# An attention pair: the next image's projection moved between the last weighted sums, bursts placed anew, and casts given to GpSimd

## The chip, the core and the metric

The kernel runs on one core of a Trainium2 chip. The core has a matrix engine (PE, whose weight loads are listed as PEld), a vector engine (DVE), a scalar engine (ACT), GpSimd (POOL), and SyncE (SP), which here only issues transfers. The metric is the device time of one execution in microseconds. Seven executions of the kernel before took 2803.36 to 2808.71 us, with a median of 2805.67.

## The reference

Eight images of 512 channels and 32x32 tokens (T = 1024) pass through two attention layers.

```python
# layer 0, 8 heads of 64 channels
h   = group_norm(x)                       # 32 groups
qkv = qkv_w @ h + qkv_b
q, k, v = split per head, each fake_quant to 8 bits over the whole tensor
w   = softmax(q k / 8);  a = w v          # per head, 1024 x 1024
x   = x + proj_w @ a + proj_b
# layer 1, one head of 512 channels
h = group_norm(x);  q, k, v = wq h, wk h, wv h
o = softmax(q k / sqrt(512)) v
x = x + wp @ o + bp
```

The range of the quantization is that of all images together, so all of q, k and v of layer 0 must be known before the first softmax.

## The kernel before

**Stages.** The first stage (to 627 us) computes q, k and v of layer 0 for all images and writes them to DRAM. The second one does the attention of image 0 alone (to 794 us), with folded weights for layer 1 being computed beside it. In the third one layer 1 of image b runs together with layer 0's attention of image b + 1. The last image's layer 1 ends the program.

**Attention of layer 0** is the generator `attention` (L744). A unit is a head pair's tile of 128 keys by 512 queries. For a unit, PE makes two score matmuls (`st`), ACT takes the exponential of the tile into `pt` (L768), a cast to 16 bits makes its high part `two[:, 0]` (L777), and DVE's subtraction makes the low part (L778). From both parts PE computes weighted sums (`av`) and row sums (`sm`). One step of the generator does four units; the text calls it a burst. It makes the scores of four units to come, two of them at its start and two in its middle or end, and the weighted and row sums of the four units that the burst before has prepared. The casts and subtractions of a burst's last two units are put off as a chore (`later("sum", ...)`) and issued at the next occasion, at the latest when the next burst begins. Score tiles (`st`) come from a PSUM pool of two double banks, `ps_s` (L631); `av` and `sm` from `ps_v`; the banks of layer 1 from `ps_o`. There are three `pt` buffers (L640).

The engine of the cast depends on where the burst is: while image 0 is alone, odd units go to DVE; in a *dense* burst (one that `others` asked for with a negative yield) the two late units go to GpSimd and DVE; all others go to ACT.

**Layer 1** is the generator `others` (L1447). For image b it runs `project` (L908; attention output times the projection weights, plus x, with the statistics of the norm taken on the way), `norm1` (L948) and `layer1` (L1243). Products are done in blocks by a scheme of seven half-sized products (`seven`, L986). A block has two PSUM banks x and y. Products 0, 2, 4 and 5 go one upon the other into x, and between them ACT copies out what x holds (`keep`); DVE adds such copies to y (`add`). After each product the block yields its step number. Layer 1 of an image has, in this order, the blocks a_block (half 0), v_block2 (0 and 1), s_block (0 and 1), o_run (half 0), a_block (half 1), s_block (0 and 1) and o_run (half 1). Products of o_run are twice as long as the others. Before its third product, o_run adds up the softmax's row sums with PE (`sm_l`), which needs DVE's sum `acc`.

**Who sets the order.** The main loop asks `others` for a step and, after each of its yields, does one burst. So the places of `yield` in `others`, `run` (L1232) and `o_run` (L1140) set where bursts lie. Before the change every block yields at step 5, o_run also at step 3, the projection between its halves, and the norm three times with -1 (dense). That makes 16 bursts per image, as many as an image of layer 0 has. `LEAD` (L42) bursts are done ahead, before layer 1 begins. Matmuls run in the order in which they are written; for the other engines a scheduler fixes an order when the program is built.

For the last image alone, `project` and `norm1` already run inside the o_run of the image before it, between its steps 4 and 6 (L1321 to L1331), with banks of `ps_v`. For all other images they come after that o_run, and the image's norm is followed by its first block.

**Loads.** The projection's weights and x of the next image are loaded by ACT's queue just before the last o_run of an image (L1313, L1314), x in eight transfers (`load_x2`, L882).

Of the kernel before, what the change touches and what calls it, by code (L numbers as in the profile page):

```python
# [40 lines left out]
ALIKE = 8.0  # L41
LEAD = 3  # L42
IN_ORDER = mybir.DependencyInfo(mybir.DependencyClass.NoSync, mybir.DependencyReason.DATA)
# [10 lines left out]
def attn_pair_kernel(  # L54
# [126 lines left out]
    flag = const.tile([P, 1], I32, name="flag")  # L181
    off = const.tile([P, 1], F32, name="off")

    with ExitStack() as fast:
# [4 lines left out]
        def av_bank(name):  # L189
            return ps_v.tile([P, 512], F32, tag="v", name=name)  # L190

        def bank(name):
# [551 lines left out]
        def attention():  # L744
# [10 lines left out]
            def scores(u, wait=False):  # L755
                b, j, hf, s = units[u]
                if hf == 0 and s == 0:
                    settle("quant")
                nm = f"{b}_{j}_{hf}"
                qt, kt, _ = pairs[b, j]  # L760
                st = pair_ps(f"st_{nm}_{s}")
                for i, r in enumerate(HALF):
                    mm(
                        st[:, i, :], lhsT=kt[r, bass.ts(s, P)],
                        rhs=qt[r, bass.ts(hf, 512)], start=True, stop=True,
                    )
                pt = ptp.tile([P, 2, 512], F32, tag="p", name=f"pt_{nm}_{s}")
                nc.scalar.activation(pt, st, AF.Exp, scale=esc)  # L768
                parts[u] = two = partp.tile([P, 2, 2, 512], F16, tag="two", name=f"two_{nm}_{s}")
                cast = nc.scalar.copy  # L770
                if alone and s % 2:
                    cast = nc.vector.tensor_copy
                elif dense and wait and not alone:
                    cast = nc.vector.tensor_copy if s % 2 else nc.gpsimd.tensor_copy

                def split():
                    cast(two[:, 0], pt)  # L777
# [75 lines left out]
            for u in range(0, len(units), 4):  # L853
                b, j, hf, s = units[u]
                settle("sum")
                if hf == 0 and s == 0:
                    n = b * PAIRS + j + 1
                    if n < B * PAIRS:
                        pairs[divmod(n, PAIRS)] = load_pair(*divmod(n, PAIRS))

                if u + 4 < len(units):
                    scores(u + 4)
                    scores(u + 5)
                weighted((u, u + 1))
                late = dense
                for n in range(2):
                    if n == late:
                        weighted((u + 2, u + 3))  # L870
                        if s == NT - 4:
                            finish(b, j, hf)
                    if n == 0 and u + 4 < len(units):
                        scores(u + 6, wait=True)
                        scores(u + 7, wait=True)
                chore(0)
                last = (j, hf, s) == (PAIRS - 1, NH - 1, NT - 4)
                yield 6.0 + (hf == NH - 1 and s == NT - 4), b + last
# [3 lines left out]
        def load_x2(b, dma):  # L882

            xts[b] = l1p.tile([P, CC, T], F32, tag="h", name=f"h2_{b}")
            for hf in range(NH):
                for oc in range(CC):
                    dma(
                        xts[b][:, oc, bass.ts(hf, 512)], x_v[b, :, oc, bass.ts(hf, 512)]
                    )

# [17 lines left out]
        def project(b, bank=bank):  # L908
# [6 lines left out]
            for hf in range(NH):  # L915
# [16 lines left out]
                if hf + 1 < NH:  # L932
                    yield 1
            for k in [k for k in ao if k[0] == b]:
# [40 lines left out]
        def inverse1(b, hf, acc):  # L975
            nm = f"l1_{b}_{hf}"
            sm = row_sums([acc[:, bass.ts(i, P)] for i in range(4)], lambda nm: pair_ps(nm)[:, 0, :], nm)
            rs = l1p.tile([P, 512], F32, tag="rs1", name=f"rs1_{b}_{hf}")
# [161 lines left out]
        def o_run(b, hf, vt, vs, ps_, pts, acc, rx, between):  # L1140
# [46 lines left out]
            for step in seven(  # L1187
# [4 lines left out]
            ):  # L1192
                if step == (3 if final else 2):
                    settle("acc")
                    rs = inverse1(b, hf, acc)
                if step == (4 if final else 3):
                    yield 1
# [4 lines left out]
                elif step == 5:  # L1202
                    if not final:
                        finish(2)
                    yield from between[1]()
                    yield 1
                elif step == 6:
                    for n in ((0, 2, 3) if final else (3,) if spare else ()):
                        finish(n)
                    settle("o")  # L1210
                    yield from between[2]()
                    if final and hf == NH - 1:
                        check_sums()
                    if (1, 0) not in rx:
                        load_x1(b, hf, 1, 0, rx)
# [15 lines left out]

        def run(*blocks):  # L1232

            for steps in zip(*blocks):
                if steps[0] == 5:
                    yield 1
# [6 lines left out]
        def layer1(b, steps):  # L1243

            for _ in steps:
# [5 lines left out]
            def a_run(hf):  # L1253
                gq = l1p.tile([P, 7, CC // 2, 256], F32, tag="g", name=f"g_{b}_{hf}")
                yield from run(a_block(b, hf, gq))
                return gq
# [22 lines left out]
            for hf in range(NH):  # L1279
# [55 lines left out]
        def fold():  # L1335
# [16 lines left out]
            def through(i):  # L1352
# [8 lines left out]
                widen(wide[:, i], z)  # L1361


            tiny = small.tile([P, 32], F16, tag="tiny", name="tiny")
            nc.vector.tensor_scalar(tiny, ones[:, 0:32], 2.0**-20, None, ALU.mult)
            ps = bank("tiny")
            for i in range(4):
                mm(ps[32 * i : 32 * i + 32, 0:32], lhsT=ones16, rhs=tiny, start=True, stop=True)
            nc.vector.tensor_scalar(off, ps[:, 0:1], 2.0**-13, None, ALU.not_equal)

# [34 lines left out]
        def check_sums():  # L1405
# [12 lines left out]
            nc.vector.tensor_scalar(bad[:, 0:1], bad[:, 0:1], -1.0, 1.0, ALU.mult, ALU.add)  # L1418
            nc.vector.tensor_max(bad[:, 0:1], bad[:, 0:1], off)
            nc.vector.tensor_reduce(bad[:, 1:2], rcs[:, NR0:], AX.X, ALU.max)  # L1420
# [417 lines left out]
```

## Time and profile before

| | |
|---|---|
| seven executions, median | 2805.67 us |
| the profiled execution | 2807.82 us |
| its span, first to last instruction | 2806.0 us |
| granted PE clock | 0.990 of full speed |
| PE busy | 2641.8 us |
| DVE busy | 1879.1 us |
| ACT busy | 1305.4 us |
| GpSimd busy | 74.7 us |
| casts of `two` on ACT, DVE, GpSimd | 430, 61, 21 |
| their mean time there | 1.07, 0.68, 2.50 us |

A line of a timeline gives the start and the length in us, the engine, the line of the kernel, the operation, the tile written and those read, the shapes, and how many instructions in a row were merged; the square bracket gives the idle time of the engine before it and what ended it. A line of the windows gives the window, its length, and the busy time of each engine with the number of its instructions; then the granted clock, the share of the DMA engines' time and GB/s. Matmuls overlap, so the distance of two starts tells more than a matmul's length. PE runs a float32 matmul as two instructions, so counts on it are twice those in the code.

### The profile page before, as it was taken

Reading aid. Unit: us, or ns where it says so; the run is one execution under the profiler, and the core shown is the slowest. Engines: PE = TensorE matmul, PEld = TensorE weight load, DVE = VectorE, ACT = ScalarE, POOL = GpSimd, SP = SyncE. Lnnn points to the kernel's source line nnn. Section 1 sums busy time; section 2 is a strip of 40 time slices with the busy share of each in tenths; the row PEclk is TensorE's granted clock in tenths of the full one; section 3 lists DMA queues with packets and bytes.
Section 4 is the critical chain, followed back from the end, with each engine's and each line's share of the span. In section 5 each row is a group of like instructions: output and inputs, shape, how many; then the busy total and the mean of one; then the engine's idle time right before and its main releaser. Section 6 shows DMA issues by size and latency. Waiting matters only on the chain.

```text
span 2806.0 us, 33124 instructions
## 1 busy us (share of the span) xinstructions
PE 2641.8 (94%) x13114; PEld 1634.8 (58%) x13114; DVE 1879.1 (67%) x2798; ACT 1305.4 (47%) x1648; POOL 74.7 (3%) x51
## 2 busy tenths in 40 slices
PE   7999999997789999999999999999999999899998
PEld 3455555552236664666466556646664666466687
DVE  6766665658986667666865676667667666755534
ACT  0011111117965665655566566556664665565021
POOL 0000000000000001000100010001001000100000
PEclk9999999999899999999999999999999999999999
DMA  5233232323321233124202411331232124202401
GB/s 195 101 120 120 111 114 90 120 110 130 100 94 31 65 99 101 46 65 132 82 26 65 158 50 39 98 129 31 65 102 99 46 65 136 65 1 54 143 8 43
DMA packets 148228, 241.93 MB, mean 86 GB/s; under 512 B 27360, under 2 KB 92896, under 8 KB 146528
## 3 DMA queue, kind: packets, MB, share of 16 engines
q1 hardware_dynamic: 116544, 181.50, 19.6%
q10 hardware_dynamic: 31520, 58.23, 6.3%
q8 instruction: 104, 1.70, 0.3%
q14 instruction: 60, 0.49, 0.1%
HBM read 152.86 MB, written 86.28 MB: 85 GB/s over the span
## 4 chain that ended last, share of the span: by engine, by line
PE 55%; DVE 17%; ACT 14%; issue 9%; DMA 4%; POOL 1%; ACTq 0%; SPq 0%; DVEq 0%; POOLq 0%
PE s L106 12%; PE qkps L106 10%; PE o L106 9%; ACT pt L768 7%; PE pj L106 7%; DVE two L778 6%; PE v2ps L106 5%; PE vps L106 5%; ACT two L777 4%; PE av L106 2%; PE g L106 2%; PE st L106 1%; PE sm L106 1%; DVE acc L1294 1%; DMA raw<-k_d 1%
## 5 line engine op out<-in xcount | busy, mean ns | idle before, releaser
L778 DVE TENSOR_TENSOR two<-pt,two 128x1024 f16<-128x1024 f32 x512 | 612.5, 1221 | 199.6 <-ACT two L777 199.0
L768 ACT ACTIVATE pt<-st,esc 128x1024 f32<-128x1024 f32 x512 | 554.0, 1128 | 198.3 <-PE st L106 182.7
L777 ACT CAST two<-pt 128x1024 f16<-128x1024 f32 x430 | 441.2, 1067 | 1.3
L106 PE MATMUL av<-two,v 128*64 128x512 f16 x2048 | 279.3, 394 | 1.6 <-DVE two L778 0.8
L396 ACT ACTIVATE u<-qkps,qkb 128x512 f32<-128x512 f32 x84 | 57.8, 688 | 476.5 <-PE qkps L106 467.5
L106 PE MATMUL s<-g,h 128*128 128x256 f32 x1024 | 237.4, 382 | 14.9 <-ACT p L1123 7.9
L106 PE MATMUL st<-q,k 64*128 64x512 bf16 x1024 | 173.6, 388 | 70.8 <-ACT pt L768 69.4
L106 PE MATMUL pj<-ao,wp 128*128 128x512 f32 x512 | 223.3, 594 | 0.1
L106 PEld LDWEIGHTS s<-g,h 128*128 128x128 f32 x1024 | 191.8, 190 | 50.4 <-ACT p L1123 10.3
L106 PEld LDWEIGHTS <-v 128*64 128x64 f16 x2048 | 97.9, 110 | 155.8 <-issue 105.1
L106 PE MATMUL s<-g,sums 128*128 128x256 f32 x768 | 179.8, 384 | 1.1 <-ACT kept_u L1094 0.7
L106 PE MATMUL o<-p,v 128*128 128x256 f32 x768 | 173.9, 383 | 5.6 <-ACT p L1123 5.6
L106 PE MATMUL qkps<-x,wqkv 128*128 128x512 f32 x352 | 164.7, 611 | 2.6 <-DVE x L155 2.6
L106 PEld LDWEIGHTS pj<-ao,wp 128*128 128x128 f32 x512 | 96.5, 190 | 119.5 <-issue 114.7
L106 PEld LDWEIGHTS o<-p,v 128*128 128x128 f32 x768 | 143.6, 190 | 35.1 <-ACT p L1123 10.8
L106 PE MATMUL sm<-two,ones 128*32 128x512 f16 x2048 | 162.3, 395 | 0.0
L106 PEld LDWEIGHTS s<-g,sums 128*128 128x128 f32 x768 | 142.4, 190 | 28.7 <-issue 6.3
L106 PEld LDWEIGHTS <-k 64*128 64x128 bf16 x1024 | 38.6, 94 | 202.6 <-issue 201.9
L106 PE MATMUL qkps<-sums,wa 128*128 128x512 f32 x336 | 153.3, 592 | 0.0
L106 PE MATMUL g<-h,wa 128*128 128x256 f32 x512 | 123.1, 389 | 15.4 <-DVE g L1070 8.2
L106 PE MATMUL v2ps<-wm,h 128*128 128x256 f32 x512 | 119.4, 382 | 6.9 <-ACT g L1057 5.3
L1127 DVE TENSOR_TENSOR p<-s,kept_u 128x512 f32<-128x512 f32 x90 | 61.7, 685 | 93.0 <-ACT kept_u L1094 86.1
(222 smaller groups left out, 3476.1 us busy)
## 6 DMA issues: line engine op xcount, KB each, us to landing
rs<-rs_d SPq DMA_DIRECT2D x80, 256.0 KB
x<-in_x_dram SPq DMA_DIRECT2D x32, 512.0 KB
raw<-q_d SPq DMA_DIRECT2D x32, 512.0 KB
raw<-k_d SPq DMA_DIRECT2D x32, 512.0 KB
raw<-v_d SPq DMA_DIRECT2D x32, 512.0 KB
x_d<-h SPq DMA_DIRECT2D x64, 256.0 KB
x<-x_d ACTq DMA_DIRECT2D x64, 256.0 KB
out_dram<-x SPq DMA_DIRECT2D x64, 256.0 KB
```

Source lines behind the costliest of these rows:

```text
L106: ins = nc.tensor.matmul(*args, **kw).ins
L396: nc.scalar.activation(dst, x, AF.Identity, bias=bias)
L768: nc.scalar.activation(pt, st, AF.Exp, scale=esc)
L777: cast(two[:, 0], pt)
L778: nc.vector.tensor_tensor(two[:, 1], pt, two[:, 0], ALU.subtract)
L1127: tt(dst, ps, u, ALU.add)
L1294: later("acc", 0, lambda two=two: tt(acc, *two, ALU.add))
```

## The change

- In every image's last o_run, between its steps 4 and 6, the next image's projection and norm are done (only image 0's stay in front). Their PSUM tiles are taken from the scores' pool `ps_s`.
- The norm no longer yields, except for image 0's. The bursts that were there are placed elsewhere: v_block2 (0) at step 3, v_block2 (1) at steps 1 and 5, the s_blocks of half 0 at 3 and at 1 and 5, those of half 1 and the a_block of half 1 at step 3, o_run at steps 3 and 6, the second one also at 1, and one, now dense, between the halves of the projection.
- Outside the stage of image 0 alone, the cast of every odd unit is done by GpSimd, that of every even one by ACT.
- A burst that is not dense does the weighted sums of all four units and then their row sums, instead of two units at a time.
- `LEAD` is 2. x is loaded in two transfers. A test of how PE treats very small 16-bit numbers (`tiny`, `off`) is dropped.

```diff
-LEAD = 3
+LEAD = 2
...
+        def score_bank(name):
+            return pair_ps(name)[:, 0, :]
...
                 cast = nc.scalar.copy
-                if alone and s % 2:
-                    cast = nc.vector.tensor_copy
-                elif dense and wait and not alone:
-                    cast = nc.vector.tensor_copy if s % 2 else nc.gpsimd.tensor_copy
+                if s % 2:
+                    cast = nc.vector.tensor_copy if alone else nc.gpsimd.tensor_copy
...
-                weighted((u, u + 1))
+                weighted((u, u + 1) if dense else range(u, u + 4))
                 late = dense
                 for n in range(2):
                     if n == late:
-                        weighted((u + 2, u + 3))
+                        if dense:
+                            weighted((u + 2, u + 3))
...
             for hf in range(NH):
-                for oc in range(CC):
-                    dma(
-                        xts[b][:, oc, bass.ts(hf, 512)], x_v[b, :, oc, bass.ts(hf, 512)]
-                    )
+                dma(xts[b][:, :, bass.ts(hf, 512)], x_v[b, :, :, bass.ts(hf, 512)])
...
                 if hf + 1 < NH:
-                    yield 1
+                    yield -1
...
-                if step == (3 if final else 2):
+                if step == 1 and hf == NH - 1:
+                    yield 1
+                elif step == (3 if final else 2):
                     settle("acc")
                     rs = inverse1(b, hf, acc)
-                if step == (4 if final else 3):
+                elif step == 3:
                     yield 1
...
                     yield from between[1]()
+                elif step == 6:
+                    yield from between[2]()
                     yield 1
-                elif step == 6:
                     for n in ((0, 2, 3) if final else (3,) if spare else ()):
                         finish(n)
                     settle("o")
-                    yield from between[2]()
...
-        def run(*blocks):
+        def run(*blocks, at=(5,)):
 
             for steps in zip(*blocks):
-                if steps[0] == 5:
+                if steps[0] in at:
                     yield 1
...
-                yield from run(a_block(b, hf, gq))
+                yield from run(a_block(b, hf, gq), at=(3,) if hf else (5,))
...
-                yield from run(*(v_block2(b, n, vt) for n in ns))
+                yield from run(*(v_block2(b, n, vt) for n in ns), at=(1, 5) if NH - 1 in ns else (3,))
...
-                    yield from run(*(s_block(b, hf, n, gq, pts, gather) for n in ns))
+                    yield from run(
+                        *(s_block(b, hf, n, gq, pts, gather) for n in ns),
+                        at=(1, 5) if NH - 1 in ns and hf == 0 else (3,),
+                    )
...
-                if b == B - 2 and last:
+                if b + 1 < B and last:
 
                     def first():
                         nonlocal ahead
-                        yield from project(b + 1, av_bank)
-                        ahead = norm1(b + 1, av_bank)
+                        yield from project(b + 1, score_bank)
+                        ahead = norm1(b + 1, score_bank)
                         next(ahead)
```

More of the change, by code (lines that the diff above doesn't have):

```diff
@@ L181, in attn_pair_kernel @@
     flag = const.tile([P, 1], I32, name="flag")
-    off = const.tile([P, 1], F32, name="off")
     with ExitStack() as fast:
@@ L976, in inverse1 @@
             nm = f"l1_{b}_{hf}"
-            sm = row_sums([acc[:, bass.ts(i, P)] for i in range(4)], lambda nm: pair_ps(nm)[:, 0, :], nm)
+            sm = row_sums([acc[:, bass.ts(i, P)] for i in range(4)], score_bank, nm)
             rs = l1p.tile([P, 512], F32, tag="rs1", name=f"rs1_{b}_{hf}")
@@ L1361, in through @@
                 widen(wide[:, i], z)
[L1364 to L1369, printed above, removed]
             for i, (rows, lw, rw) in enumerate(((wa_rows, NQ1, NK1), (wm_rows, NV1, WP1))):
@@ L1418, in check_sums @@
             nc.vector.tensor_scalar(bad[:, 0:1], bad[:, 0:1], -1.0, 1.0, ALU.mult, ALU.add)
-            nc.vector.tensor_max(bad[:, 0:1], bad[:, 0:1], off)
             nc.vector.tensor_reduce(bad[:, 1:2], rcs[:, NR0:], AX.X, ALU.max)
```

## The prediction

> **Names.** A *burst* is one step of the attention generator: scores of four tiles (st), weighted sums and row sums of the four before (av, sm). a0, a1, v0, v1, s00, s01, s10, s11, o0, o1 are the blocks of seven products of layer 1 in their order, s01 the second score block of half 0. *Step n* is `yield n` in `seven` (L986). A *round* runs from one image's projection to the next one's.
>
> **What bounds it now.** I read the page first: which engine is full?
>
> ```profile
> PE 2641.8 (94%) x13114; PEld 1634.8 (58%) x13114; DVE 1879.1 (67%) x2798; ACT 1305.4 (47%) x1648; POOL 74.7 (3%) x51
> ```
>
> PE bounds the whole, and no other engine is near full. So the change is worth what it does to PE's own work and to PE's waits. The windows by round (span, then busy time and count of PE, PEld, DVE, ACT, POOL) give a typical round:
>
> ```profile
> 1060.97:1324.39 263.42, 248.55 (x1397) 158.17 (x1396) 179.48 (x236) 158.13 (x198) 9.39 (x4) 1.00 0.26 80
> ```
>
> The idle column of PE's timeline in it adds up to 14.9 us. Next, a burst, in PE's timeline and then in ACT's:
>
> ```profile
> 1139.79 0.61 PE L106 MATMUL st<-q,k 64*128 64x512 bf16 x4
> 1140.33 1.05 PE L106 MATMUL av<-two,v 128*64 128x512 f16 x8
> 1141.31 0.62 PE L106 MATMUL sm<-two,ones 128*32 128x512 f16 x8
> 1141.86 1.05 PE L106 MATMUL av<-two,v 128*64 128x512 f16 x8
> 1142.84 0.62 PE L106 MATMUL sm<-two,ones 128*32 128x512 f16 x8
> 1143.39 0.60 PE L106 MATMUL st<-q,k 64*128 64x512 bf16 x4
> 1143.93 1.99 PE L106 MATMUL v2ps<-wm,sums 128*128 128x256 f32 x8
> ```
>
> ```profile
> 1140.38 2.12 ACT L768 ACTIVATE pt<-st,esc 128x1024 f32<-128x1024 f32 x2
> 1142.38 2.00 ACT L777 CAST two<-pt 128x1024 f16<-128x1024 f32 x2
> 1144.27 2.14 ACT L768 ACTIVATE pt<-st,esc 128x1024 f32<-128x1024 f32 x2
> ```
>
> By the starts the burst takes 4.14 us. Four av pairs take 0.98 and two st pairs 0.54, so a pair is 0.22 and each change of kind costs 0.54 - 0.44 = 0.10. Third, what a block costs that has no burst at step 5 (end of image 6, attention done, ACT idle): product 5 goes on in the bank that step 5's copy (L1017) is still reading.
>
> ```profile
> 2590.21 1.89 PE L106 MATMUL s<-g,h 128*128 128x256 f32 x8
> 2592.83 1.99 PE L106 MATMUL s<-g,sums 128*128 128x256 f32 x8 [0.73 <-ACT kept_u L1094]
> ```
>
> Fourth, GpSimd's few casts in the norm stretch, and what DVE does at the end of the third:
>
> ```profile
> 1104.03 1.04 POOL L777 CAST two<-pt 128x1024 f16<-128x1024 f32 x1 [4.55 <-ACT pt L768]
> 1107.43 1.39 POOL L151 TENSOR_TENSOR grstd_b<-grstd_b,mhalf 128x4 f32<-128x4 f32 x1 [2.36 <-DVE grstd_b L150]
> 1111.79 5.76 POOL L777 CAST two<-pt 128x1024 f16<-128x1024 f32 x1 [2.97 <-ACT pt L768]
> ```
>
> ```profile
> 1115.97 0.68 DVE L972 TENSOR_TENSOR sums<-h,sums 128x512 f32<-128x512 f32 x1
> 1116.58 1.25 DVE L155 TENSOR_SCALAR h<-h,gmean_b,grstd_b 128x512 f32<-128x512 f32 x1
> ```
>
> A cast takes 1.04 where DVE pauses, and 5.76 where DVE runs back to back (it does from 1108.93 on); when the cast gets through, DVE pays: 1.25 where the same instruction takes 0.53 a little later. Fifth, the norm stretch on PE:
>
> ```profile
> 1105.90 0.39 PE L106 MATMUL st<-q,k 64*128 64x512 bf16 x2 [1.03 <-ACT pt L768]
> ...
> 1118.48 1.99 PE L106 MATMUL g<-h,wa 128*128 128x256 f32 x8 [1.21 <-DVE g L1070]
> ```
>
> **What it saves.** The built kernels' static order has 110 bursts beside layer 1 (109 before), 100 of them undivided.
>
> S1. An undivided burst (st, 16 av, 16 sm, st) has two changes of kind less: 4.14 - 0.20 = 3.94; 100 x 0.20 = 20.0.
>
> S2. The norm stretch: from 1092.70 to 1111.09 PE needs 18.4 us for three bursts and two 0.34 matmuls that are 13.1 without waits; with the waits of 0.48 and 1.21 in a0 that is 7.0. It goes for images 1 to 6 (image 7 had it already): 42.0.
>
> S3. Bursts in score blocks take 4.55, as the second exp is behind a cast and a p-exp on ACT. In the new order the odd cast is off ACT: 4 x 0.41 x 7 rounds = 11.5.
>
> S4. Waits at block edges that follow a burst at step 5, where ACT comes late to the last copy: v0-v1 0.23, a1-s10 0.73, s10-s11 1.32 + 0.37, s11-o1 0.49, in a1 0.58, and the second sm_l, which a burst at o1's step 1 will cover, 1.25: 4.97 x 7 = 34.8.
>
> S5. LEAD 2: one burst leaves the stage where ACT sets the pace (764.00 to 771.07 is one burst, 7.07): 3.1.
>
> Sum 111.4.
>
> **What it costs.**
>
> C1. Seven blocks lose their burst at step 5 and wait there for ACT's copy: v0, s00, s10, s11, o0 at 0.73; a1 copies in two activates (0.84 for 0.59): 0.98; in o1 a norm matmul lies in the gap: 0.4. 5.03 x 7 = 35.2.
>
> C2. The same blocks then need step 5's DVE add for product 6, and DVE does the burst's four subtractions (1.14 each) first. Worked out for a burst in whose middle ACT also copies av and sm (L815, L816): exps 0.59 to 2.71, cast to 3.6, copies to 4.6, exps to 6.7, cast to 7.75; DVE's third and fourth subtraction to 10.1, the add to 10.75. PE: 3.94 + 2 x 1.78 (products 3, 4), copy to 8.25, product 5 to 10.03. Late by 0.75: v0, s11; 0.5 in a1; in v1 (step 1) 0.55 at product 3; in s00 two quantizations (0.74) come between: 0.4, or 1.4 if the odd cast then waits for DVE; I take 1.1. 3.65 x 7 = 25.6; from 10.5 (half of the late adds hidden) to 62 (each behind one more cast of 1.05).
>
> C3. v1-s00 0.85 for 0.26; s01 has two bursts, the second in the old ACT order, its last st 0.9 late; a0-v0 0.5 better; the first sm_l: between s01's first burst and it DVE has eight subtractions, 11 us of other work and two odd casts that it must let through, which makes 3.1 of the 1.59. 2.5 x 7 = 17.5; 10 to 25.
>
> C4. The projection in o1 uses the scores' two buffers: in its burst the second st waits for DVE's evacuation of the last pj (0.75 + 0.2, less the first st): 0.8; at step 6 it waits for grstd: 0.84. Then a0: DVE has the norm (four 0.48, sums 0.6 each), two subtractions and one odd cast ahead of o1's last add, which frees a0's second bank: 2.05, and 0.35 two products on. 4.05 x 6 = 24.3; 10 (a0 hidden by product 6) to 33.
>
> C5. Image 0 keeps its norm stretch, with one cast more on ACT per burst: 0.95 x 3 = 2.9; 0 to 6.
>
> C6. A cast that starts just ahead of a DVE instruction holds it up; the row is 0.72. Six adds a round end waits of PE; for half of them: 2.1 x 7 = 14.7; 0 to 44 (1.05 for each).
>
> Sum 120.2, between 66 and 205. No end can be excluded: the trace of before never has a cast on GpSimd beside a score or o block. I take the middle values, nearer to the 5.76 row than to the 1.04 row wherever DVE runs back to back.
>
> By the Trainium skill (SBUF — State Buffer, SBUF: two separate sides) the port pair that DVE and GpSimd share goes whole to whichever starts first, so a cast should be late by one DVE instruction at most: 1.04 + 1.22 = 2.3 us, an estimate. With that the odd-cast shares of C2 to C4 would go (about 18 us), and the sum would end at 2797. The row of 5.76 behind some seven DVE instructions says otherwise.
>
> **Costed at nothing.** The loads of x: eight issues on ACT (4.14 us together at 2597.96) become two; at 0.53 each, as the two-run load of x1, ACT is free 3 us sooner in o1, but PE's next wait there was DVE's. They must land 22 us before the projection needs them (three o products of 3.56, sm_l and two bursts, one product more); at image 6 the projection came 16 us after the first issue and waited for nothing. If late, up to 5 us a round. GpSimd's pow comes behind one cast (1.04), in C4. The dropped `off` test is four matmuls and some DVE work at 625: under 1 us. On SP the projection's eight stores of x1 (0.32 each, L930) now stand among o1's stores of out; behind them wait the next pair's raw loads, needed a burst later: at most 1 us a round, taken as nothing.
>
> **Sum.** The profiled execution took 2807.82 (span 2806.0 and 1.8 around it), 2.15 over the median of 2805.67. 2807.8 - 111.4 + 120.2 = 2816.6; against the median, 2814.5.
>
> **Rivals.** A measurement of this kernel tells about 0.2% from no change, that is 2800 to 2811.
>
> *Faster:* casts slip into DVE's pauses (DVE is busy 179 of 263 us a round), so that only C1 and the ACT-bound part of C2 to C4 stay. Costs near 85 give 2780; all at the low end, 2760. For it: the first two casts of each norm stretch took 1.0 to 1.2; against: the third took 5.6 to 5.8 in six rounds. It decides where a round's new waits and late adds stay under 14 us.
>
> *No change:* costs near the savings, 2806.
>
> *Much slower:* DVE becomes the bound of the s01-o0 stretch and of a0; every odd cast costs it 1.05 (32 x 1.05 on 179.5 is 211 of 263), each late add is behind one: 2850. For it: sm_l already ends on DVE; against: 50 us of slack.
>
> That the change does not do what it says is out: the static order has 218 casts on GpSimd (21 before), 256 on ACT (430), and each later projection at o1's step 4.
>
> **Chances.** Forecast 0.36, no change 0.18, faster 0.34, much slower 0.12. So faster 0.34, same 0.18, slower 0.48. Range 2772 to 2852: the faster case without its end, the much slower one up to its price. The forecast's own range is 2811 to 2830.
>
> **What would show it.** S1: bursts of 3.94. S2: no wait of PE for st in a norm stretch after image 0. C1: 0.7 before product 5, ended by ACT kept_u, in seven blocks. C2, C4: waits of g, v2ps and s that DVE ends. C3: sm_l waits near 3. Casts: a mean above 2 us, the longest above 4. PE idle in a round near 19. Wrong if casts stay near 1.1, or if ACT waits for x1's loads in front of exps.

## The result, and the profile after

The changed kernel takes 2816.28 us (median of 13 runs, 2810.45 to 2827.38), the kernel before, run beside it, 2805.16 us (34 runs, 2800.83 to 2812.59). The ratio is 1.0045, with a 95% interval of 1.0035 to 1.0054: 0.45% slower, well clear of the 0.2% that can be told from no change. The forecast was 2814.5 us. As a difference from the kernel before, 8.8 us were forecast and 12.6 came by the ratio.

The profiled execution took 2820.18 us, 3.9 above the median; its span is 2818.4. The line of busy times on the changed kernel's page, which answers to the first one shown of before:

```profile
PE 2626.3 (93%) x13110; PEld 1653.1 (59%) x13110; DVE 1924.2 (68%) x2772; ACT 1152.0 (41%) x1474; POOL 281.5 (10%) x248
```

PE is busy 15.5 us less than before, and yet the span is 12.4 us longer. So the loss is waiting. I summed PE's idle gaps over each trace, and, after the first product of image 0's projection, the gaps above 60 ns by the engine that ended them. The records of the granted clock give a third sum: each stretch at 0.5 loses half its length of PE's work, and that loss is part of the busy time.

| us | before | after | difference |
|---|---|---|---|
| span | 2806.0 | 2818.4 | +12.4 |
| all idle gaps of PE | 156.4 | 184.3 | +27.9 |
| PE busy, without the clock loss | 2612.7 | 2590.7 | -22.0 |
| clock loss | 29.1 | 35.7 | +6.6 |
| gaps that ACT ended, layer 1's part | 66.6 | 50.8 | -15.8 |
| gaps that DVE ended, layer 1's part | 32.1 | 80.3 | +48.2 |

That is the change in short: PE has 22 us less to do, waits 16 us less for ACT and 48 us more for DVE.

A typical round by the windows (window, its length, then busy time and count of PE, PEld, DVE, ACT, POOL, the clock, and two figures of the DMA):

```profile
1055.58:1321.53 265.95, 248.27 (x1397) 162.61 (x1396) 186.27 (x233) 135.27 (x173) 39.55 (x34) 0.99 0.25 79
```

ACT is down to 135 us of 266, DVE up to 186 although the round has three DVE instructions fewer. PE's idle gaps in the round are 17.7 us; the prediction had near 19.

Next, PE's timeline around half 0's o block in this round:

```profile
1209.65 3.83 PE L106 MATMUL o<-p,v 128*128 128x256 f32 x17
1216.20 0.42 PE L106 MATMUL sm_l<-acc,ones 128*32 128x128 f32 x8 [2.71 <-DVE acc L1293]
1216.55 5.38 PE L106 MATMUL o<-g,vsum 128*128 128x256 f32 x16
1221.86 0.60 PE L106 MATMUL st<-q,k 64*128 64x512 bf16 x4
1222.40 1.92 PE L106 MATMUL av<-two,v 128*64 128x512 f16 x16
1224.24 1.05 PE L106 MATMUL sm<-two,ones 128*32 128x512 f16 x16
1225.22 0.61 PE L106 MATMUL st<-q,k 64*128 64x512 bf16 x4
1225.76 1.56 PE L106 MATMUL o<-p,v 128*128 128x256 f32 x6
```

The burst takes 3.90 us by its starts, 4.14 in the one shown of before. The first sm_l waits 2.71 us for DVE, 1.59 before in this round (the prediction said 3.1). And the product just after it, 16 matmuls, takes 5.38 us where the same product takes 3.62 elsewhere. The windows of the granted clock (the third figure from the end) say why:

```profile
1213.11:1216.53 3.42, 0.71 (x10) 0.16 (x8) 3.03 (x5) 0.00 (x0) 0.00 (x0) 1.00 0.00 0
1216.53:1219.94 3.41, 3.41 (x12) 2.76 (x9) 0.18 (x1) 0.27 (x1) 0.00 (x0) 0.50 0.03 1
1219.94:1223.35 3.41, 3.41 (x23) 2.06 (x24) 0.00 (x0) 1.38 (x2) 0.00 (x0) 1.00 0.25 44
```

In the 3.41 us after the stretch that holds the wait, PE has half its clock. The wait cost its 2.71 us and 1.7 us more. This price is in none of the prediction's terms.

The other new waits, PE's timeline at the second product of image 1's a0 and in s00:

```profile
1109.45 2.16 PE L106 MATMUL g<-h,wa 128*128 128x256 f32 x7 [2.02 <-DVE kept_u L1159]
...
1177.78 1.89 PE L106 MATMUL s<-g,h 128*128 128x256 f32 x8
1180.35 1.99 PE L106 MATMUL s<-g,sums 128*128 128x256 f32 x8 [0.68 <-ACT kept_u L1092]
1183.63 3.72 PE L106 MATMUL s<-g,h 128*128 128x256 f32 x16 [1.29 <-DVE p L1125]
```

The first is C4, the second C1 and the third C2, at nearly the sizes foretold (2.05, 0.73 and 1.1). Last, the casts (duration as minimum, median, maximum):

```profile
L777 ACT CAST two<-pt x256: 1028/1052/1103, 638.6 to 2564.6; 128x1024 f16<-128x1024 f32 x128
L777 POOL CAST two<-pt x218: 1026/1042/2143, 799.2 to 2564.7; 128x1024 f16<-128x1024 f32 x109
```

On GpSimd they take 1.04 us in the median, 2.14 at most and 1.20 on average. The prediction wanted a mean above 2 and a longest above 4: no cast waited for DVE for longer than about one DVE instruction.

### The profile page after: what moved, and what is told of

It is laid out like the page before. It is cut to its first block, busy times and chain, and to the rows that moved or that the text cites. A ratio compares the mean times of both kernels' runs of the same rounds, so it can differ in the third digit from the quotient of the medians.

```text
span 2818.4 us, 33256 instructions
## 1 busy us (share of the span) xinstructions
PE 2626.3 (93%) x13110; PEld 1653.1 (59%) x13110; DVE 1924.2 (68%) x2772; ACT 1152.0 (41%) x1474; POOL 281.5 (10%) x248
## 4 chain that ended last, share of the span: by engine, by line
PE 54%; DVE 22%; ACT 10%; issue 6%; DMA 5%; POOL 1%; ACTq 0%; SPq 0%; DVEq 0%; POOLq 0%
PE qkps L106 12%; PE s L106 10%; DVE two L778 9%; PE o L106 7%; PE vps L106 6%; ACT pt L770 5%; PE pj L106 5%; PE v2ps L106 4%; PE g L106 4%; ACT two L777 3%; PE av L106 3%; DMA rs<-rs_d 2%; PE st L106 2%; PE sm L106 1%; DVE h L155 1%
## 5 line engine op out<-in xcount | busy, mean ns | idle before, releaser
L778 DVE TENSOR_TENSOR two<-pt,two 128x1024 f16<-128x1024 f32 x512 | 617.7, 1237 | 260.9 <-ACT two L777 246.5
L777 POOL CAST two<-pt 128x1024 f16<-128x1024 f32 x218 | 261.6, 1200 | 1545.9 <-ACT pt L770 1545.9
L777 ACT CAST two<-pt 128x1024 f16<-128x1024 f32 x256 | 269.9, 1054 | 1.1
L106 PE MATMUL av<-two,v 128*64 128x512 f16 x2048 | 256.2, 388 | 0.2
L106 PE MATMUL st<-q,k 64*128 64x512 bf16 x1024 | 166.8, 387 | 56.3 <-ACT pt L770 41.7
L106 PEld LDWEIGHTS <-v 128*64 128x64 f16 x2048 | 104.4, 110 | 134.2 <-issue 62.3
L106 PEld LDWEIGHTS s<-g,sums 128*128 128x128 f32 x768 | 142.0, 190 | 49.8 <-ACT kept_u L1092 22.7
L106 PE MATMUL sm<-two,ones 128*32 128x512 f16 x2048 | 142.1, 388 | 0.0
```

Of the source, the lines that this page charges most:

```text
L106: ins = nc.tensor.matmul(*args, **kw).ins
```

## The experiments

Ratios are to runs of the kernel before on the same chip; a difference in us is that of two ratios times 2805.

| kernel | median us | ratio, 95% interval | gaps ended by ACT, DVE | clock loss |
|---|---|---|---|---|
| changed | 2816.28 | 1.0045 (1.0035 to 1.0054) | 50.8, 80.3 | 35.7 |
| step5 | 2836.83 | 1.0110 (1.0094 to 1.0125) | 45.8, 88.0 | 49.1 |
| act_casts | 2841.51 | 1.0142 (1.0126 to 1.0158) | 103.6, 36.6 | 49.3 |
| norm_front | 2884.90 | 1.0297 (1.0275 to 1.0319) | 103.9, 64.5 | 52.2 |
| pairs | 2824.14 | 1.0074 (1.0061 to 1.0088) | 44.4, 63.9 | 38.9 |
| sm_late | 2804.06 | 0.9995 (0.9985 to 1.0004) | 52.0, 66.2 | 26.6 |
| img0 | 2815.10 | 1.0039 (1.0027 to 1.0050) | 49.8, 78.7 | 28.1 |
| before | 2805.16 | 1 | 66.6, 32.1 | 29.1 |
| undiv | 2798.04 | 0.9975 (0.9965 to 0.9985) | 77.5, 34.1 | 25.7 |
| before_sm | 2790.54 | 0.9946 (0.9934 to 0.9958) | 70.1, 14.9 | 25.7 |
| casts_alone | 2827.08 | 1.0072 (1.0058 to 1.0087) | 59.4, 55.2 | 28.2 |
| sm_undiv | 2772.51 | 0.9884 (0.9866 to 0.9901) | 72.9, 19.2 | 19.7 |
| three | 2796.52 | 0.9963 (0.9951 to 0.9976) | 63.2, 45.9 | 28.2 |
| casts_vs | 2765.15 | 0.9856 (0.9840 to 0.9873) | 64.6, 16.0 | 26.1 |

The six below the changed kernel take parts of the change back or mend one place in it; the last six do parts of it, or the same mend, on the kernel before.

### step5: five bursts back at step 5

```diff
-                yield from run(a_block(b, hf, gq), at=(3,) if hf else (5,))
+                yield from run(a_block(b, hf, gq), at=(5,))
...
-                yield from run(*(v_block2(b, n, vt) for n in ns), at=(1, 5) if NH - 1 in ns else (3,))
+                yield from run(*(v_block2(b, n, vt) for n in ns), at=(1, 5) if NH - 1 in ns else (5,))
...
-                        at=(1, 5) if NH - 1 in ns and hf == 0 else (3,),
+                        at=(1, 5) if NH - 1 in ns and hf == 0 else (5,),
```

> The changed kernel with the one burst of v0, s00, s10, s11 and a1 back at step 5 (the second bursts of v1, s01 and o1 stay, and all else). The prediction's terms: C1 goes in five blocks (4 x 0.73 + 0.98 = 3.9 a round), C2 goes in v0, s11, a1 and s00 (0.75 + 0.75 + 0.5 + 1.1 = 3.1), and of S4 the edges v0-v1, a1-s10, s10-s11 and a1 come back (0.23 + 0.73 + 1.69 + 0.58 = 3.2): 3.8 x 7 = 26.6 us less than the changed kernel, 2789 to 2790. Theory 1: the edge waits came from casts on ACT, and every odd cast is off ACT now, so they do not come back, and it ends 40 to 50 us below the changed kernel, near 2771. Theory 2: the edges come back and the late additions only move to another product; then it stays at 2810 to 2820.

It is 18 us slower than the changed kernel; none of the three had that. C1's waits went as worked out (s waits that ACT ends fell from 17.8 to 10.9 us, those of v2ps that DVE ends from 8.9 to 1.0). But s11's burst at step 5 and o1's at step 1 are now three products apart, and PE runs into a wait for DVE there. PE's timeline in this kernel, at o1's burst:

```profile
1303.39 1.56 PE L106 MATMUL av<-two,v 128*64 128x512 f16 x10
1308.27 1.49 PE L106 MATMUL av<-two,v 128*64 128x512 f16 x6 [3.31 <-DVE two L778]
```

Waits of av for DVE are 19.9 us in all (none in the changed kernel). With the waits that went, PE's gaps grow by only 3.5 us in sum, but the clock loss grows by 13.4: most of the 18. Theory 2 has the mechanism, that lateness only moves, but not the price. In this order step 3 is worth its C1, as the bursts of s11 and o1 then lie further apart and av waits for nothing.

### act_casts: odd casts back on ACT

```diff
-                if s % 2:
-                    cast = nc.vector.tensor_copy if alone else nc.gpsimd.tensor_copy
+                if s % 2 and alone:
+                    cast = nc.vector.tensor_copy
```

> The changed kernel with the odd casts, after the stage of image 0 alone, on ACT instead of GpSimd. The prediction's terms: C6 goes (14.7 us) and so do the shares of odd casts in C2 to C4 (about 18 us), S3 is lost (11.5 us): 21 us less, 2795. Rival, from the trace of the changed kernel, where the 218 casts took 1.20 us on average and at most 2.14: the casts cost the path next to nothing, and ACT's second pair of exps comes a cast later in every burst; then it is slower than the changed kernel by 10 to 40 us, 2826 to 2856, and PE shows waits for ACT pt in the score blocks.

It is 27 us slower than the changed kernel: the rival. PE's timeline in v0, and ACT's up to the copy that the product waits for:

```profile
1399.77 1.89 PE L106 MATMUL v2ps<-wm,h 128*128 128x256 f32 x8
1404.04 1.99 PE L106 MATMUL v2ps<-wm,sums 128*128 128x256 f32 x8 [2.39 <-ACT kept_u L1092]
```

```profile
1399.47 2.16 ACT L770 ACTIVATE pt<-st,esc 128x1024 f32<-128x1024 f32 x2
1401.47 2.03 ACT L777 CAST two<-pt 128x1024 f16<-128x1024 f32 x2
1403.35 0.64 ACT L1092 COPY kept_u<-v2ps 128x512 f32<-128x512 f32 x1
```

With the burst at step 3, the copy that product 5 needs stands behind the burst's last two exps and its casts on ACT. The wait of C1, 0.68 in the changed kernel, is 2.39 here. The same wait comes in v0 of seven rounds and in s11 of six, and after 6 of these 13 (not after the one shown) the clock is halved for a stretch. So the casts on GpSimd are what keeps C1 at the price that I took from a place where ACT was idle. The gaps swap: 52.8 us more for ACT, 43.7 less for DVE.

The same DVE instructions are busy 1868.6 us here and 1924.2 in the changed kernel: 55.6 us for 218 casts, 0.26 each. It falls on some instructions more than on others; DVE's quantization of k has much of it (changed kernel first, then this one):

```profile
L655 DVE TENSOR_SCALAR k<-raw,bhi x32: 742/748/1531, 628.2 to 2447.3; 128x1024 bf16<-128x1024 f32 x32
```

```profile
L655 DVE TENSOR_SCALAR k<-raw,bhi x32: 744/746/750, 627.8 to 2462.5; 128x1024 bf16<-128x1024 f32 x32
```

### norm_front: projection and norm back in front

```diff
-                if step == 1 and hf == NH - 1:
-                    yield 1
-                elif step == (3 if final else 2):
+                if step == (3 if final else 2):
...
-                if b + 1 < B and last:
+                if b == B - 2 and last:
```

The second bursts of v1 and s01 are out as well (`(5,)` in place of `(1, 5)`).

> The changed kernel with the projection and the norm of images 1 to 6 back in front of their own layer 1, with three dense bursts in the norm, and without the extra bursts at step 1 of v1, s01 and o1. The prediction's terms: S2 is lost (42 us), the second sm_l waits again (1.25 x 7 = 8.8), C4 goes (24.3), and of C2 and C3 what the extra bursts cost (0.55 in v1, 0.9 and 1.5 in s01: 20.7): 5.8 us more, 2822. Rival: with the casts as they are now the norm stretch is dearer than it was before, as image 0's shows (its waits of the dense bursts and of the first g come to 12.4 us where they were 8.4): 24 us more again, about 2846. Second rival: C4 was dearer than I took it, and the projection in front is no loss: 2805 or less.

It is 71 us slower than the changed kernel, far beyond all three. Part of that has nothing to do with the question. PE's timeline in o1, and the issues on ACT's queue beside it:

```profile
1594.47 3.62 PE L106 MATMUL o<-g,vsum 128*128 128x256 f32 x16
1602.09 3.18 PE L106 MATMUL o<-p,vsum 128*128 128x256 f32 x9 [4.00 <-ACT kept_u L1188]
```

```profile
1594.67 0.34 ACTq L904 DMA_DIRECT2D wm<-wm_d  x1
1600.21 0.55 ACTq L1228 DMA_DIRECT2D x<-x_d  x1
1600.80 0.61 ACTq L904 DMA_DIRECT2D wm<-wm_d  x1
1601.45 0.58 ACT L1188 COPY kept_u<-o 128x512 f32<-128x512 f32 x1 [7.36 <-issue]
```

The loads of wm now stand in front of o1's copy on ACT, and ACT does nothing for 7.36 us. PE's gaps of 3.39 to 4.26 in six rounds come to 23 us. What is left holds the rival's mechanism: st waits that ACT ends are 40.7 us against 8.8, and the longest of them, 1.70, comes in every norm stretch, as in image 0's of the changed kernel. With these casts, then, the stretch in front is dear, which speaks for S2's sign. How much S2 is worth by itself this kernel doesn't settle.

### pairs and undiv: the undivided sums taken back, and alone

```diff
-                weighted((u, u + 1) if dense else range(u, u + 4))
+                weighted((u, u + 1))
...
-                        if dense:
-                            weighted((u + 2, u + 3))
+                        weighted((u + 2, u + 3))
```

> The changed kernel with the weighted sums of a burst in two pairs of units again, each followed by its row sums. The prediction's S1: two changes of kind more in each of 100 bursts, 0.10 us each: 20 us more, 2836, with bursts of 4.14 us on PE again. Rival: the parts of the later two units are needed 1.1 us later by PE, which takes waits away elsewhere, so that less than half of it is seen: below 2826.

The other way round on the kernel before:

> The kernel before with the weighted sums of a burst that is not dense undivided, and nothing else changed; 88 bursts. The prediction's S1: 88 x 0.20 = 17.6 us less, 2787. Theory from the run with pairs, where PE was busy 26 us longer but idle 25 us less: undividing saves PE's time in full, and two thirds of it come back as waits for DVE and ACT, which have as much to do as before: 2798 to 2802.

With pairs it is 8 us slower than the changed kernel (0.29%); undivided sums alone make the kernel before 7 us faster (0.25%). Both lie where the rival and the theory had them. The page of pairs:

```profile
PE 2652.8 (94%) x13110; PEld 1635.9 (58%) x13110; DVE 1919.0 (68%) x2772; ACT 1152.9 (41%) x1474; POOL 271.6 (10%) x248
```

Pairs cost PE 26.5 us of busy time, 3.3 of them clock loss; 23 us for 100 bursts is S1's mechanism and more than its 20.0. But PE's idle gaps fall from 184.3 to 159.0. In undiv it is the reverse: 12.3 us of new gaps, for 15.7 us of work saved. So S1 is right for PE's work and more than twice too large in time. ACT and DVE have as much to do as ever, and where a wait ends on them, PE only comes to it earlier. In undiv this can be seen: the bursts in score blocks take 4.55 us as before, and the waits of st for ACT grow from 32.5 to 45.5 us, which is as much as all its new gaps.

### sm_late and before_sm: the row sums one product later

```diff
-                elif step == (3 if final else 2):
+                elif step == 3:
                     settle("acc")
                     rs = inverse1(b, hf, acc)
-                elif step == 3:
-                    yield 1
+                    if not final:
+                        yield 1
```

> The changed kernel with sm_l (and its settling of acc) one product later in every o block, at step 3 ahead of that step's burst, as the last image has it already. In the changed kernel's trace o0's sm_l waits 2.71 us in each of seven rounds (19.0 us), and in six of them the granted clock is 0.5 in the 3.41 us just after (seven such stretches of 1.7 us lost each, 11.9 us). Theory: PE's idle time in a stretch lowers the granted clock in the next one, so a long wait costs more than its length; with the wait behind a product of 3.56 us both go: 2816.3 - 19.0 - 11.9 = 2785, and the clock loss of the whole run falls from 35.7 to about 24 us. Rival A: the clock has nothing to do with that wait; 2797, with the clock loss unchanged. Rival B: the wait only moves on, because DVE's work and rs are late for the scaling at step 4 and 5: 2805 to 2816.

The same on the kernel before, where the burst of step 3 follows it as well:

> The kernel before with sm_l one product later, at step 3 ahead of the burst. Its sm_l waits are 1.0 to 1.6 us each, 15.3 us in all, and no stretch of clock 0.5 follows one of them. Theory: all of the 15.3 us go, and nothing more: 2789 to 2791, with the clock loss as before (29 us). Rival: DVE's sum is late by more than the trace shows at step 2 and the wait moves on to the scaling: above 2798.

The changed kernel becomes 14 us faster and is level with the kernel before. PE's timeline of the same place in sm_late, a round later:

```profile
1473.36 3.62 PE L106 MATMUL o<-g,vsum 128*128 128x256 f32 x16
1476.90 0.43 PE L106 MATMUL sm_l<-acc,ones 128*32 128x128 f32 x8
1477.26 0.39 PE L106 MATMUL st<-q,k 64*128 64x512 bf16 x2
```

No wait, and the product takes its 3.62 us again. The sm_l gaps fall from 19.0 us to nothing and the clock loss from 35.7 to 26.6, which rules out rival A. But 5.4 us come back as waits of the projection for DVE; in all, PE's gaps fall by 13.1. Theory had 31 us; 14 came. (The two profiled executions differ by 20.9, but they lie 3.9 above and 4.8 below their medians.) DVE's lateness was not all at this place.

In the kernel before the gain is 15 us, as the theory had it: the 15.3 us of sm_l gaps go and DVE has slack behind them. This single line is worth more than the whole change lost. But as it gains about as much in either kernel (14 and 15 us), its waits don't make the difference between the two.

### img0: image 0's norm stretch with the casts of before

```diff
+                if first and dense and wait:
+                    cast = nc.vector.tensor_copy if s % 2 else nc.gpsimd.tensor_copy
-                if s % 2:
+                elif s % 2:
```

(`first` is true until the first yield that isn't negative.)

> The changed kernel with the casts of before in the dense bursts around image 0's projection and norm alone (late even ones on GpSimd, late odd ones on DVE, the others on ACT). The prediction's C5 (2.9 us) has only the casts on ACT in it, so 2813. From the changed kernel's trace, where the first g waited 7.37 us for h after 4.69 before and the st waits were 5.0 for 3.8: 4 to 6 us less, 2810 to 2812. Rival: image 0's round is slower for what follows in it, and the stretch has no part in that: 2816.

It is 1.7 us faster, and the intervals overlap: the rival. The first g still waits 6.16 us (7.37 in the changed kernel, 4.69 before), so these casts are only a small part of that wait. C5's small price stands; the first round's 6.9 us over before stay in part unexplained (it holds two bursts more and three o products of 3.56 less, and 3.4 us more of clock loss).

### casts_alone: the odd casts on GpSimd, nothing moved

```diff
                 elif dense and wait and not alone:
                     cast = nc.vector.tensor_copy if s % 2 else nc.gpsimd.tensor_copy
+                elif s % 2 and not dense:
+                    cast = nc.gpsimd.tensor_copy
```

> The kernel before with the odd casts of its bursts that are not dense on GpSimd, and nothing moved; dense bursts keep their casts. The prediction's terms: S3 (11.5) and the ACT waits at block edges of S4 (v0-v1, a1, a1-s10, s10-s11, s11-o1: 3.72 x 7 = 26.0) are saved, C6 (14.7) is paid: 22.8 us less, 2783. Theory from the run with all casts back on ACT, which was 25 us slower than the changed kernel: the casts are worth about that anywhere, 2775 to 2785, with casts near 1.2 us on average. Rival: the changed kernel needs them only because its bursts lie elsewhere; here ACT's lateness was covered, and it stays at 2800 or above.

It is 20 us slower than the kernel before, where all but the rival had a gain of 20 to 30, and the rival none. PE's timeline in s10, with the burst in it:

```profile
1516.13 1.99 PE L106 MATMUL s<-g,h 128*128 128x256 f32 x8 [0.23 <-ACT g L1059]
1518.82 1.99 PE L106 MATMUL s<-g,h 128*128 128x256 f32 x8 [0.70 <-DVE g L1072]
...
1526.02 0.61 PE L106 MATMUL st<-q,k 64*128 64x512 bf16 x4
...
1529.62 0.39 PE L106 MATMUL st<-q,k 64*128 64x512 bf16 x2
1530.24 0.39 PE L106 MATMUL st<-q,k 64*128 64x512 bf16 x2 [0.24 <-ACT pt L768]
1530.57 1.99 PE L106 MATMUL s<-g,sums 128*128 128x256 f32 x8
```

The burst still takes 4.55 us with its last st waiting, though the odd casts of such bursts have left ACT. ACT's timeline beside it:

```profile
1526.61 1.12 ACT L768 ACTIVATE pt<-st,esc 128x1024 f32<-128x1024 f32 x1
1527.62 0.63 ACT L1125 ACTIVATE p<-p 128x512 f32<-128x512 f32 x1
1528.13 1.04 ACT L779 CAST two<-pt 128x1024 f16<-128x1024 f32 x1
1529.07 1.13 ACT L768 ACTIVATE pt<-st,esc 128x1024 f32<-128x1024 f32 x1
```

The second exp is still behind a p-exp and a cast, but the cast is that of an even unit, which stays on ACT. The burst takes 4.55 in undiv too, and 3.90 in the changed kernel at step 3, where ACT does the two exps in a row. So S3's cause was wrong: the wait goes with the place at step 5, not with the odd cast. The edges that ACT ended do shrink (a1-s10's 0.73 is 0.23, s10-s11's 1.32 is 0.38), but one product after the first of them DVE ends a wait of 0.70. In all 7.2 us less for ACT, 23.1 more for DVE, whose instructions got longer by 56.4 us for 174 casts more (0.32 each).

### sm_undiv, three, casts_vs: parts put together on the kernel before

sm_undiv joins the edits of before_sm and undiv, three adds that of casts_alone, and casts_vs has in its place

```diff
+                elif s % 2 and light:
+                    cast = nc.gpsimd.tensor_copy
```

where `light` is set for the bursts that v and s blocks yield.

> The kernel before with sm_l one product later and the weighted sums undivided. If both gains add up (15.0 and 7.5 us): 2783. If undividing only brings PE sooner to waits for ACT, of which there are more now that sm_l's wait is gone: 2788 to 2791, no better than sm_l alone.

> The kernel before with sm_l one product later, the weighted sums undivided, and the odd casts of bursts that are not dense on GpSimd; no burst, projection or norm is moved. If the gains add up (15.0, 7.5 and 22 to 25): 2758 to 2761, faster than both kernels, and it is the moves that cost the changed kernel its gain. If casts and undividing compete for the same waits: 2765 to 2783. Rival: casts hold DVE up where a wait of PE ends on DVE: above 2783.

> The kernel before with sm_l one product later, the weighted sums undivided, and the odd casts on GpSimd only in bursts that lie in v and s blocks; in a and o blocks, in the projection and in dense bursts the casts stay as before. Theory: casts on GpSimd cost time where PE waits for DVE (with all of them there the first g of a1 waits 3.75 us for DVE's x, and g and v2ps after an a block's burst 0.7 to 0.8 for DVE) and save some where it waits for ACT (edges of v and s blocks, 0.4 to 0.8 us each, 1.75 a round): 12 us less than with no such casts (2772.5), 2760; at least not slower than that. Rival: a cast on GpSimd costs DVE about 0.27 us wherever it is, and that sets the pace of the following o block too: 2780 to 2790, between no cast moved (2772.5) and all (2796.5).

sm_undiv is 33 us faster than the kernel before, 10 more than the sum of its parts. Against undiv, PE's gaps are 20.7 us fewer: the sm_l gaps (8.8), and with them the waits of the projection for DVE (3.9) and of st for ACT (4.9), and 6 us of clock loss. I had expected the sum or less. That the earlier sm_l takes those other waits with it is what the traces show; why, I haven't tested.

With the odd casts on GpSimd in all bursts that are not dense, three loses 22 us of that: the rival. PE's timeline at the end of o0 and a1's first products:

```profile
1490.11 3.62 PE L106 MATMUL o<-g,v 128*128 128x256 f32 x16
1497.48 2.93 PE L106 MATMUL g<-h,wa 128*128 128x256 f32 x6 [3.75 <-DVE x L1174]
```

DVE's scalings at the end of o0, which free a1's bank, come late (waits of 1.2 to 3.8 us in the seven rounds, none in sm_undiv). casts_vs keeps the casts out of the a and o blocks and the projection, and this wait is gone. The same place in it, and its busy times:

```profile
1480.06 3.62 PE L106 MATMUL o<-g,v 128*128 128x256 f32 x16
1483.51 3.62 PE L106 MATMUL g<-h,wa 128*128 128x256 f32 x16
```

```profile
PE 2616.4 (95%) x13114; PEld 1653.2 (60%) x13114; DVE 1894.8 (69%) x2798; ACT 1229.0 (44%) x1568; POOL 163.4 (6%) x131
```

Its gaps that ACT ended are 8.4 us below those of sm_undiv, those that DVE ended 3.2 below. It takes 2765.15 us, ratio 0.9856 (0.9840 to 0.9873): 1.4% faster than the kernel before and 1.9% faster than the changed one. Its interval and that of sm_undiv touch, so it is not shown to beat that; that it is not slower, against 22 us lost with all casts, is what tells the theory from its rival. Nor does a cast cost DVE the same everywhere: DVE is busy 11.3 us longer than in sm_undiv for 80 casts more, 0.14 each, where casts_alone had 0.32.

Five of the ratios lead from the kernel before to the changed one, a part at a time: sm_l one product later, -15 us (before_sm); sums undivided, -17 (sm_undiv); odd casts on GpSimd, +22 (three); the moves, with `LEAD`, the loads, the dropped test and the casts of the dense bursts, +9 (sm_late against three); sm_l back in its place, +14 (the changed kernel). On this path the casts and the moves make the change a loss. The parts don't simply add, though: with the bursts where the changed kernel has them, the same casts save 27 us (act_casts).

## Why the prediction was right, and which steps were not

The time and the sign were right: 2816.6 was forecast for the profiled execution and 2820.2 came; the medians are 1.8 us apart, and 8.8 us of loss were forecast where 12.6 came. The sum got there partly by errors that cancel, so that it came this close is in part luck.

- **S1** (20.0). Right as work: bursts of 3.90, and 23 us of PE's time. Wrong as time: the runs with and without give 7 to 8 us. The step that failed is taking PE's saved work off the end, burst by burst, where the next wait ends on DVE or ACT.
- **S2** (42.0). After image 0 no norm stretch has st waits that ACT ends. It has no price by itself, as norm_front mixes in the stall of ACT's queue.
- **S3** (11.5). The bursts in score blocks did become shorter, all but s01's second, which is still at step 5 and takes 4.55. The cause given, the odd cast off ACT, is refuted by casts_alone: it is the place at step 3.
- **S4** (34.8). The waits at v0-v1, a1-s10, s10-s11 and the second sm_l are gone.
- **S5** (3.1) was not tested alone. The stage that ends at the projection took 8.3 us less with one burst less, where the burst was priced at 7.07 there.
- **C1** (5.03 a round). Measured in the round from 1321.5: 0.68 four times, 0.80, 0.99 and 0.56, together 5.07. But act_casts shows that this price holds only with the casts off ACT.
- **C2** (3.65). Measured 1.01, 0.27, 1.29, 0.49 and 0.34, together 3.40.
- **C3** (2.5). sm_l was 2.71 for the 3.1 foretold, and six of the seven sm_l waits bring a stretch of half clock that C3 didn't have. Without the wait sm_late gained 14 us, not the 19.0 of its gaps and not the 31 with the clock: part of DVE's lateness comes back at the projection (5.4 us).
- **C4** (4.05). The first wait of the projection's burst is not 0.8 but 0.6 to 1.6, with a second of 0.99 that I had not seen; grstd's is 0.41 for 0.84, a0's 1.7 to 2.0 for 2.05, and the 0.35 after it didn't come. On average 4.14 a round: the sum was right, its parts were not.
- **The odd casts' shares in C2 to C4** (about 18). The step that failed in its reason. They had the casts wait for DVE, and in the changed kernel none waited for long; the longest took 2.14 us. The waits that they were to lengthen came near the sizes foretold all the same (s00's add 1.29, sm_l 2.71, a0 about 1.8), with DVE late. That the casts have a part in it, act_casts suggests, where sm_l waits 1.73; but there PE also waits more for ACT ahead of it.
- **C6** (14.7). Its mechanism is what the runs show: DVE is held up by the casts, 0.26 us a cast on average, 55.6 us in all. How much of that reaches PE's path no run tells by itself. In the changed order the casts are still a good bargain (27 us), because ACT's copy is what product 5 waits for; in the order before they are a bad one (20 us against).
- **Not in the sum:** the clock, 6.6 us, and a wait of some 0.54 for DVE at a1's first product, in each of seven rounds.

The sign "wrong if casts stay near 1.1" therefore came: the mean was 1.20, the median 1.04. By the prediction's own words the cast terms were wrong, in what waits for what. The gaps of C1, C2 and C4 came at about their sizes; S1 fell some 12 us short, and the clock took 6.6. Against these stand S2 and C6, which no run prices alone, so the sum can't be closed term by term.

On the rule of the Trainium skill (SBUF — State Buffer, SBUF: two separate sides), the lock on the shared ports goes for one whole instruction to whoever starts first. The estimate of 2.3 us that the prediction worked out from it for the slowest cast fits the 2.14 of the changed kernel; in norm_front the slowest took 2.58. But the rows of 5.76 were no accident of one trace: before, undiv, before_sm, sm_undiv, casts_alone, three and casts_vs, which all keep the norm's casts of before, have six casts of 5.6 to 5.8 us each. There the measurement goes against the estimate, by which a cast waits for one DVE instruction at most, and the prediction was wrong only in carrying those rows over to the new places. What lets a cast through in one place and not in the other stays open. The lengthened DVE instructions (k's quantization up to 1.53 for 0.75) are the other side of it.

## What to carry to other kernels

Work taken off the full engine is worth its length only where the next wait isn't set by another engine: list PE's gaps by who ends them, and price a saving from the stretch behind it. Moving a cast to another engine helps where PE waits for the engine that it leaves, and costs where PE waits for the one that it disturbs; with the odd casts of all its bursts but the dense ones moved the kernel before lost 20 us, and with only those of the v and s blocks moved sm_undiv lost nothing. A wait of 2 us and more can be dearer than it looks, by the clock in the stretch behind it. And look for a wait that one line removes: the row sums one product later did more here than the change.

## What the runs showed of the hardware

The granted clock of PE went down after pauses of 2 us, which the prediction had left out of its sum. The records change on a grid of 3.41 us. In the 14 profiled executions, between the first and the last projection, I compared PE's idle time in each stretch at full clock with the clock of the next. With 1.95 us idle or more, 80 of 81 were followed by a stretch at 0.5; with 1.7 to 1.95 us, 6 of 35; with 1 to 1.7 us, 7 of 334; below 1 us, none of 7026. Each such stretch costs 1.7 us of PE's work, half its length. Whether a wait of 2.7 us has that price depends on how it lies on the grid, which shifts from run to run: the seven sm_l waits of 2.71 were followed by half clock in six rounds. It goes with the scatter of the times, too: of the changed kernel's runs the four at a mean clock of 0.986 took 2822 to 2827 us, the two at 0.990 took 2811.6 and 2813.1.

The Trainium skill (TensorE: Matmul & The Clock Gate, HAM oscillation — how this bites in real kernels) gives as a rule that PE should have no idle gap above some 3.4 us. The measurement decides here: 2.0 to 2.7 us idle in a stretch were enough.

A GpSimd cast of 128x1024 lengthened DVE's work by 0.14 to 0.32 us on average (0.26 in the changed order, 0.32 in the order before, 0.14 with casts in v and s blocks alone). Between act_casts and the changed kernel it falls on the quantizations (L652, L655), the subtractions (L778), the norm's scaling (L155), the scalar_tensor_tensors from SBUF (L832, L1169) and a few others, where the longest took some 0.8 us more, and hardly on DVE's additions such as acc (L1293), which took 0.69 and 0.68 us.
